# Pre-layernorm attention with an FP8 projection: reciprocals by exp(-ln), pieces spread over rounds, elementwise work on another engine

## Chip, cores and metric

The kernel runs on one core of a Trainium2 chip. The metric is the device time of one execution, in microseconds, as the median of several runs. The engines are named as in the profile: PE (matmul; PEld is its weight load), DVE (vector), ACT (scalar, with activation functions), POOL (GpSimd) and SP, which here only issues DMAs.

## What is computed

Two batches of 2048 rows of 512 numbers pass through attention with 16 query heads and 2 key/value heads of 32 dimensions, with rotary embedding, and then through a projection whose operands are rounded to 8-bit floats. Cut to what matters:

```python
def reference(x, wq, bq, wk, bk, wv, bv, wo, bo, weight):
    h = layernorm(x)
    q, k, v = h @ wq + bq, h @ wk + bk, h @ wv + bv      # 16, 2, 2 heads of 32
    q, k = rope(q) * 32 ** -0.5, rope(k)
    scores = einsum("bqhd,bkhd->bhqk", q, repeat(k)) * 32 ** -0.5
    out = einsum("bhqk,bkhd->bqhd", softmax(scores), repeat(v))
    x = x + out @ wo + bo
    a, sa = quant_e4m3(layernorm(x).reshape(-1, 512))    # one scale for the whole tensor
    w, sw = quant_e4m3(weight)
    return x + (a @ w.T * (sa * sw)).astype(bfloat16)
```

## The kernel before

**Blocks, quads, units, rounds.** The 4096 rows are 8 blocks `n` of 512 rows (4 per batch). A block has 4 quads of heads, and a quad two halves of 256 queries: 64 units `u`, which the main loop takes one after the other. A unit goes over the 2048 keys in 16 chunks of 128, in 4 rounds `r` of 4 chunks. For a chunk `probabilities` (L964 to L988) puts the scores of four heads into one of two PSUM tiles `T` (two matmuls at L978; in the first two chunks four more at L969 subtract the row maxima) and ACT writes `p = exp(T)` (L987). As there are two tiles, the third chunk's matmuls wait for the first chunk's exponential. `weigh` multiplies the probabilities of the *previous* round with the values (L924), so that PE has work between the second and the third chunk.

**Sums of the softmax.** DVE adds the probabilities of two chunks (`add_pair`, L961). The pair of chunks 0 and 1 lies in a `pair` buffer, of which there are two, and an accumulating DMA that POOL issues adds it to the pair of chunks 2 and 3 (`accumulate`, L991). `join` (L994) adds what two rounds left, and PE sums over the keys with a matrix of ones (L942) in the rounds of the next unit. `finish_heads` (L891 to L921) then copies the sums on ACT (L895), takes their maximum for a later check (L897), takes reciprocals in two pieces on DVE (L903) and multiplies on POOL (L904).

**Maxima of the next unit.** In rounds 0 and 1 `first_scores` computes the scores against the first 128 keys and DVE their maxima (L517); in round 3, between the second and the third chunk, `gather_maxima` transposes them on PE and copies them on ACT (`mT`, L533).

**Everything else** is cut into jobs: Python generators that yield the kind of their next step (ON_PE, ON_DVE, OTHER, LATER). Jobs project keys and values of a later block (`project_kv`), queries of the next block (`project_q`), and the output of the previous block (`finish_block`, then `second_norm`). The loop calls `fill(kind, pieces)` at fixed places, which runs the next step of a job that is due: one ON_PE piece in rounds 0 and 1 and two in rounds 2 and 3, as long as there are any. All jobs borrow one PSUM bank (`bank`, `give_back`). Since each engine runs its instructions in the order of the program, a step lands on each engine between the loop's own instructions.

**In a job.** Rotary embedding swaps halves of each head by 8 small DMAs on SP (`swapped`, L304), rotates on DVE two rounds later (`turn`: `rotate`, L309) and multiplies and adds on POOL (`rope`, L325 and L326). `halves` splits a tile into a rounded high part (ACT, L236) and a low part (POOL, L237). For queries this is done in `stack_queries` at the start of a unit, which stores both parts to DRAM and reads them back spread over partitions. The normalisation of a later block's rows is done on ACT with two instructions per tile (L250, L253). `ask` starts the loads of a block at its first unit; where a buffer or a query isn't ready, `take_x` and `stack_next` run further steps at once (`advance`). The bias `bo` is added to the 512 rows of residual by one accumulating DMA of 1 MB on POOL's queue (`add_bias`, L548).

Of the kernel before, what the change touches and what calls it, by code (L numbers as in the profile page):

```python
# [16 lines left out]
P = 128  # L17
# [10 lines left out]
def preln_attn_fp8_ffn_kernel(  # L28
# [54 lines left out]
    LATER = "later"  # L83
    BACK = HB
# [22 lines left out]
    lent = [None]  # L107

# [12 lines left out]
    def give_back():  # L121
        if attending[0]:
            lent[0] = None

# [23 lines left out]
    def load_tables(n):  # L148
        blk = n % NB
        if attending[0] or n == 0:  # L150
            csb = cs.tile([P, 2, TB], F32, tag="cs", name=f"cs_{n}")
        else:
            csb = papool.tile([P, 2, TB], F32, tag="pa", name=f"cs_{n}")
        nc.sync.dma_start(csb[:, 0, :], cos_t[:, blk * TB : (blk + 1) * TB])
        nc.sync.dma_start(csb[:, 1, :], sin_t[:, blk * TB : (blk + 1) * TB])
        return csb
# [28 lines left out]
    def layernorm_stats(src, mean, rstd, name, tiles=range(NT)):  # L185
# [9 lines left out]
        engine = nc.gpsimd if attending[0] else nc.vector  # L195
        engine.tensor_scalar(var[:, at], mv[:, at, 1], EPS, None, ALU.add)
        engine.tensor_copy(mean[:, at], mv[:, at, 0])
# [33 lines left out]

    def halves(src, rows, name):
# [4 lines left out]
        nc.gpsimd.tensor_tensor(lo[:rows], src, hi[:rows].bitcast(F32), ALU.subtract)  # L237
# [6 lines left out]
    def normalized(n, xt, xnT, name):  # L244


        def normalize(i):
            if attending[0]:
                xn = t2(f"xn_{name}_{i}")
                nc.scalar.activation(  # L250
                    xn, xt[:, i, :], AF.Identity, bias=neg_mean[:, i : i + 1]
                )
                nc.scalar.activation(xn, xn, AF.Copy, scale=rstd1[:, n, i : i + 1])  # L253
                return xn
# [12 lines left out]
        if attending[0]:  # L267
            neg_mean = small.tile([P, NT], F32, tag="neg_mean", name=f"neg_mean_{name}")
            nc.scalar.mul(neg_mean, mean1[:, n, :], -1.0)
        for i in range(0, NT, 2):  # L270
            xn = {}
            for h in (i, i + 1):
                yield OTHER if attending[0] else ON_DVE
# [13 lines left out]
    def product(dst, lhs, rhs, chunks=DC):  # L287

        for c in range(chunks):
            yield ON_PE  # L290
# [32 lines left out]
    def rope(dst, q, u, rows, csb):  # L323

        nc.gpsimd.tensor_tensor(q[:rows], q[:rows], csb[:rows, 0, :], ALU.mult)  # L325
        nc.gpsimd.tensor_tensor(dst, u[:rows], q[:rows], ALU.add)  # L326
# [37 lines left out]
    def project_kv(n, xt, xnT, csb):  # L364
# [5 lines left out]
        if b not in vX:  # L370
            vX[b] = wide.tile([P, NTS, GROUPS, HD], F32, tag="vX", name=f"vX_{b}", bufs=2)
        pk = bank(f"pk_{n}")
# [3 lines left out]
        else:  # L376
            nc.gpsimd.tensor_copy(kx[:, :BACK], kx[:, TB:])
# [16 lines left out]
        if attending[0]:  # L394
            beside.insert(0, Job(stack_keys(n, kv, u, csb), due=step[0] + 2))
# [3 lines left out]
    def stack_keys(n, kv, u, csb):  # L399
# [5 lines left out]
        if attending[0]:  # L405
            table_users[0] -= 1
        cols = slice(blk * TB, (blk + 1) * TB)
        yield OTHER
        src = t2(f"dk_{n}")[:KD]
        nc.gpsimd.tensor_tensor(src, kx[:, BACK:], kx[:, :TB], ALU.subtract)  # L410
# [16 lines left out]
    q_raw = {}  # L427

    def project_q(n, xnT, csb):
        for m in range(QUADS):  # L430
            pq = bank(f"pq_{n}_{m}")
# [3 lines left out]
            raw = wide.tile([P, TB], F32, tag="q", name=f"q_{n}_{m}", bufs=QUADS + 1)  # L435
            nc.scalar.activation(raw, pq, AF.Identity, bias=bq_sb[:, m : m + 1])
            give_back()
            if attending[0]:
                u = swapped(raw, P, f"q_{n}_{m}")
                beside.insert(0, Job(turn(n, m, raw, u, csb), due=step[0] + 2))  # L440
            else:
                u = yield from rotated(raw, csb, f"q_{n}_{m}")
                rope(raw, raw, u, P, csb)
                q_raw[n, m] = raw
                table_users[0] -= attending[0]

    def turn(n, m, raw, u, csb):
# [4 lines left out]
        q_raw[n, m] = raw  # L452
# [7 lines left out]
    def stack_queries(k):  # L460

        n, quad = quads[k]
        hi, lo = halves(q_raw.pop((n, quad)), P, f"q_{n}_{quad}")
        qst[k] = wide.tile([P, 4, TB], F32R, tag="qst", name=f"qst_{k}", bufs=2)
        far = dram.tile([P, 2, TB], F32, tag=f"q_far_{k % 2}", name=f"q_far_{k}")
        for h, part in enumerate((hi, lo)):
            nc.sync.dma_start(far[:, h, :], part.bitcast(F32))
        far = far.rearrange("(j d) h t -> d h j t", j=4)
# [77 lines left out]
    def add_bias(xt):  # L546
        rows = bo.partition_broadcast(P).unsqueeze(1).broadcast_to([P, NT, D])
        nc.gpsimd.dma_start(out=xt, in_=rows, accum_op=ALU.add)  # L548

    def add_output(n, xt, attn, i, dims=range(DC)):  # L550

        po = bank(f"po_{n}_{i}_{dims[0]}")
# [135 lines left out]
    with tc.manual_schedule():  # L688
# [16 lines left out]
        assert (0, 0) in q_raw  # L705
# [16 lines left out]
    class Job:  # L722


        def __init__(self, steps, kind=None, due=0, tables=False):
            self.steps = steps
            self.tables = tables
# [8 lines left out]
        def step(self):  # L736
            if self.kind is not None:
                self.tables = False
            self.kind = next(self.steps, None)
            if self.kind == LATER:  # L740
                self.due = step[0] + 1
                self.kind = next(self.steps)

    step = [0]
    NEVER = 10**9
    queue = [Job(q0, ON_PE)]
    owner = [queue[0]]
    table_users[0] = QUADS - sum((0, m) in q_raw or m == 0 for m in range(QUADS))
# [4 lines left out]
    def fill(kind, pieces=1):  # L753

        for _ in range(pieces):
            ready = [job for job in queue if job.due <= step[0] and not job.waits()]
            if lent[0] is not None:
                ready = [job for job in ready if job is owner[0]]
# [16 lines left out]

    seen = const.tile([P, len(units)], F32, tag="seen", name="seen")
    without_x = {}
    x_res = {}
    x_taken, x_done, x_asked = [], set(), set()
# [9 lines left out]
    def take_x(name):  # L789

        while len(x_taken) >= 3 and x_taken[-3] not in x_done:
            advance()
        x_taken.append(name)

# [4 lines left out]
    def later(project, n, x, *makes):  # L799
# [3 lines left out]
        table_users[0] = QUADS if project is project_q else 1  # L803
        csb = load_tables(n)
        yield from project(n, x, *made, csb)
# [3 lines left out]
    def stack_next(u):  # L809
# [3 lines left out]
        if half == 0:  # L813
            if k + 1 < len(quads) and k + 1 not in qst:
                while quads[k + 1] not in q_raw:
# [17 lines left out]
    def start(job):  # L833
        job.due = step[0] + 1

    def load_residual(n):
        x_res[n] = xpool.tile([P, NT, D], F32, tag="x", name=f"x_res_{n}")
        load_by_halves(x_res[n], x_in[n], lambda: unbiased.append(n))
# [6 lines left out]

    def ask(u):

        k, half = units[u]

        for m in unbiased:  # L850
            add_bias(x_res[m])
            biased.add(m)
            if m in without_x:
                without_x.pop(m).due = step[0] + 2
        unbiased.clear()
        n, quad = quads[k]
        if half == 0 and quad == 0:
# [567 lines left out]
```

## Time and profile before

| | |
|---|---|
| median of 3 runs | 1808.78 us (1807.12 to 1813.49) |
| profiled execution | 1806.86 us, span of its instructions 1805.0 us |
| before the first exponential of the loop | 98 us |
| main loop, 64 units | 98 to 1689 us |
| after the loop (scale, 8-bit projection, output) | 1690 to 1805 us |
| granted TensorE clock, mean | 0.966 (0.99 in the loop) |
| busy in 98:1690 of 1592 us | PE 1485, ACT 1126, DVE 1178, POOL 509 us |

An engine's row in a timeline gives its start, its length, the engine, the source line, the operation, the tile written and read, shapes and count; in brackets stands how long the engine was idle before it, and what ended that. A row of the groups gives the number of instructions, then their busy time in us and the mean length of one in ns, then the idle time before them by what ended it.

### The profile page before, as it was taken

The page shows a single profiled execution, that of the slowest core. Times are in us where ns is not written, and L with a number is a line of the kernel's source. Part 1 is how long each engine was busy: PE and PEld are TensorE (multiplying, and loading weights), DVE is VectorE, ACT ScalarE, POOL GpSimd, SP SyncE. Part 2 cuts the span into 40 slices and gives each one's busy share as a digit, 9 for nine tenths or more (in the row PEclk, how much of TensorE's full clock was granted, in tenths as well). Part 3 has the DMA queues.
Part 4 walks back from the last instruction along what each step waited for, and adds up shares of the span by engine and source line. Part 5 has one row for each costly group of instructions (what it writes and reads, how often), then busy time and mean ns, then how long its engine had stood idle before and what let it go on. Part 6 is the DMA issues. An engine that isn't in the chain of part 4 may idle for free.

```text
span 1805.0 us, 33804 instructions
## 1 busy us (share of the span) xinstructions
PE 1598.6 (89%) x13483; PEld 916.2 (51%) x13483; DVE 1315.7 (73%) x1526; ACT 1208.3 (67%) x1473; POOL 545.2 (30%) x552
## 2 busy tenths in 40 slices
PE   5588999899998999898999998999899988899664
PEld 3254555555555555555555554555555545555322
DVE  4547787767876787767768777787878787577697
ACT  2167677876767776776766777767777667566365
POOL 2333333244322532243314222332324223122100
PEclk9699999999999999999999999999999999999878
DMA  5676676767577866767588567766677558776222
GB/s 187 175 165 134 155 151 152 179 147 158 119 189 168 171 131 150 196 157 160 121 206 167 123 141 175 161 145 128 135 186 155 120 132 182 146 183 140 64 82 107
DMA packets 105431, 272.65 MB, mean 151 GB/s; under 512 B 15536, under 2 KB 16176, under 8 KB 102576
## 3 DMA queue, kind: packets, MB, share of 16 engines
q0 software_dynamic: 40944, 142.10, 42.1%
q1 hardware_dynamic: 61904, 126.92, 23.3%
q8 instruction: 108, 1.77, 0.4%
q10 hardware_dynamic: 2416, 1.38, 0.2%
q14 instruction: 59, 0.48, 0.1%
HBM read 87.36 MB, written 40.89 MB: 71 GB/s over the span
## 4 chain that ended last, share of the span: by engine, by line
PE 50%; DVE 14%; DMA 12%; issue 10%; ACT 7%; POOL 4%; SPq 2%; ACTq 0%; DVEq 0%; POOLq 0%
PE T L978 17%; PE avs L924 16%; DMA pa<-pa 9%; ACT p L987 6%; PE po L291 5%; DVE pa L961 4%; PE pq L291 3%; PE avs L942 2%; PE T L969 2%; DVE pa L994 2%; SPq L304 2%; DMA sw_q<-q 2%; PE pk L291 2%; PE s L509 1%; DVE v L229 1%
## 5 line engine op out<-in xcount | busy, mean ns | idle before, releaser
L987 ACT ACTIVATE p<-T 128x1024 f32<-128x1024 f32 x1024 | 991.9, 1023 | 218.1 <-PE T L978 214.3
L961 DVE TENSOR_TENSOR pa<-p,p 128x1024 f32<-128x1024 f32 x511 | 687.6, 1348 | 383.0 <-ACT p L987 273.2
L978 PE MATMUL T<-qst,dkS 128*128 128x512 f32 x2048 | 688.2, 446 | 44.8 <-ACT p L987 44.4
L991 POOL DMA_DIRECT2D pa<-pa x255 | 221.0, 867 | 971.8 <-DVE pa L961 671.6
L924 PE MATMUL avs<-p,vX 128*32 128x256 f32 x8192 | 497.3, 383 | 0.0
L978 PEld LDWEIGHTS T<-qst,dkS 128*128 128x128 f32 x2048 | 343.7, 191 | 285.2 <-ACT p L987 157.6
L924 PEld LDWEIGHTS avs<-p,vX 128*32 128x32 f32 x8192 | 240.4, 110 | 228.0 <-issue 96.5
L994 DVE TENSOR_TENSOR pa<-pa,pa 128x1024 f32<-128x1024 f32 x125 | 169.8, 1358 | 0.0
L291 PE MATMUL po<-wo_sb,attn 128*128 128x512 f32 x256 | 126.1, 604 | 0.0
L903 DVE RECIPROCAL both<-both 128x128 f32<-128x128 f32 x128 | 121.4, 949 | 5.6 <-DVE seen L897 0.5
L969 PE MATMUL T<-mT,sel 128*128 128x256 f32 x512 | 102.7, 324 | 11.2 <-ACT p L987 10.7
L291 PE MATMUL pq<-xnT_q,wq_sb 128*128 128x512 f32 x224 | 112.1, 607 | 0.0
L942 PE MATMUL avs<-pa,ones 128*32 128x256 f32 x1048 | 81.5, 385 | 28.7 <-DVE pa L994 27.7
L969 PEld LDWEIGHTS T<-mT,sel 128*128 128x128 f32 x512 | 78.0, 193 | 46.0 <-issue 20.6
L509 PEld LDWEIGHTS s<-dkS,qst 128*128 128x128 f32 x512 | 79.0, 196 | 22.2 <-DVE mx L517 10.9
L517 DVE TENSOR_REDUCE mx<-s 128x4 f32<-128x512 f32 x128 | 87.4, 683 | 2.8 <-PE s L509 2.8
L1012 ACT COPY both<-avs 128x256 f32<-128x256 f32 x64 | 23.9, 373 | 90.8 <-PE avs L942 88.1
L509 PE MATMUL s<-dkS,qst 128*128 128x128 f32 x512 | 74.4, 269 | 9.4 <-DVE mx L517 9.4
L904 POOL TENSOR_TENSOR attn<-both 128x256 f32<-128x256 f32 x64 | 78.9, 1232 | 9.7 <-DVE both L903 9.7
L895 ACT COPY both<-avs 128x256 f32<-128x256 f32 x64 | 23.9, 373 | 84.8 <-PE avs L942 84.8
L326 POOL TENSOR_TENSOR q<-sw_q,q 128x512 f32<-128x512 f32 x30 | 54.7, 1825 | 38.3 <-DVE sw_q L309 37.9
L533 ACT CAST mT<-mtp 128x256 fp32r<-128x256 f32 x64 | 23.8, 372 | 56.5 <-PE mtp L529 56.5
(124 smaller groups left out, 1075.5 us busy)
## 6 DMA issues: line engine op xcount, KB each, us to landing
pa<-pa POOLq DMA_DIRECT2D x255, 512.0 KB, 5.0
qst<-q_far SPq DMA_DIRECT2D x128, 256.0 KB, 4.9
q_far<-hi_q SPq DMA_DIRECT2D x32, 256.0 KB, 2.8
q_far<-lo_q SPq DMA_DIRECT2D x32, 256.0 KB, 3.4
x_res<-in_L_attn_x_dram SPq DMA_DIRECT2D x16, 512.0 KB, 7.2
x_res<-in_L_attn_bo_dram POOLq DMA_DIRECT2D x8, 1024.0 KB, 12.7
out_dram<-v SPq DMA_DIRECT2D x16, 512.0 KB, 2.8
sw_q<-q SPq DMA_DIRECT2D x240, 32.0 KB, 3.6
```

The costliest lines, as they stand in the source:

```text
L291: nc.tensor.matmul(dst, lhs(c), rhs(c), start=(c == 0), stop=(c == chunks - 1))
L509: nc.tensor.matmul(s[:, j, :], qst[k][:, j, at : at + P], stacked["dkS"][:, group(k), :FIRST], start=True, stop=True, skip_group_check=True,)
L517: nc.vector.tensor_reduce(mx[:, i, :], s, AX.X, ALU.max)
L903: nc.vector.reciprocal(piece, piece)
L924: nc.tensor.matmul(av[j * HD : (j + 1) * HD, :], vX[batch(k)][:, kc, group(k), :], p[:, j, :], start=(kc == 0), stop=(kc == NTS - 1), tile ...
L942: nc.tensor.matmul(dst[j * HD : (j + 1) * HD, :], ones, part[:, j, :], start=start and i == 0, stop=stop and i == len(parts) - 1, tile_pos ...
L961: nc.vector.tensor_tensor(pa, a, b, ALU.add)
L969: nc.tensor.matmul(T[:, j, :], sel[:, j, :], maxima[u], start=(j % 2 == 0), stop=True, skip_group_check=True,)
L978: nc.tensor.matmul(T[:, j : j + 2, :], stacked["dkS"][:, group(k), kc * P : (kc + 1) * P], qst[k][:, j : j + 2, half * HB : (half + 1) * H ...
L987: nc.scalar.activation(p, T, AF.Exp, scale=SCALE)
L991: nc.gpsimd.dma_start(out=to, in_=of, accum_op=ALU.add)
L994: nc.vector.tensor_tensor(to, to, of, ALU.add)
```

## The change

Reciprocals: ACT copies the sums and adds them up in the same instruction (`accum_out`), then computes ln and exp of the negated result as a first guess; DVE makes one Newton step with three instructions, of which the last multiplies with the values. The steps are at least a round apart.

Jobs: a `product` no longer yields ahead of its first matmul, its callers do. `pieces` hands out one ON_PE piece in a round, and two in rounds 2 and 3 when more is owed than the rest of the block's rounds hold. No piece of a product starts in the round in which the bank was given back. An ON_DVE step may run while another job holds the bank.

Engines: within the loop rope, low halves, key differences, the statistics' small steps and the normalisation go to DVE (the normalisation as one instruction); before the loop POOL keeps them.

Loads: one list of what is wanted and from which unit on, two units ahead of the block; a load is taken when a buffer is free, and nothing is advanced for it. Tables of a key job lie in the tile of its normalised rows and are loaded after the transposes; tables of a query job are loaded with its first query. Queries are split and stored when they have been turned (`put_away`), a round later; `stack_queries` only reads. The bias goes to each of a block's four row tiles by a DMA of 256 KB.

Buffers: `pair` 3 for 2, `q` 2 for 5, `both` 3 rows for 2.

```diff
+            given[0] = step[0]
...
-    def load_tables(n):
+    def load_tables(n, of=None):
         blk = n % NB
-        if attending[0] or n == 0:
+        if of is not None:
+            csb = wide.tile([P, 2, TB], F32, tag=of, name=f"cs_kv_{n}")
+        elif attending[0] or n == 0:
...
+    def elementwise():
+
+        return nc.vector if attending[0] else nc.gpsimd
...
-        nc.gpsimd.tensor_tensor(lo[:rows], src, hi[:rows].bitcast(F32), ALU.subtract)
+        elementwise().tensor_tensor(lo[:rows], src, hi[:rows].bitcast(F32), ALU.subtract)
...
             if attending[0]:
                 xn = t2(f"xn_{name}_{i}")
-                nc.scalar.activation(
-                    xn, xt[:, i, :], AF.Identity, bias=neg_mean[:, i : i + 1]
-                )
-                nc.scalar.activation(xn, xn, AF.Copy, scale=rstd1[:, n, i : i + 1])
-                return xn
...
         for c in range(chunks):
-            yield ON_PE
+            if c > 0:
+                yield ON_PE
...
-        nc.gpsimd.tensor_tensor(q[:rows], q[:rows], csb[:rows, 0, :], ALU.mult)
-        nc.gpsimd.tensor_tensor(dst, u[:rows], q[:rows], ALU.add)
+        elementwise().tensor_tensor(q[:rows], q[:rows], csb[:rows, 0, :], ALU.mult)
+        elementwise().tensor_tensor(dst, u[:rows], q[:rows], ALU.add)
...
+            csb = load_tables(n, "xnT")
             beside.insert(0, Job(stack_keys(n, kv, u, csb), due=step[0] + 2))
...
-            raw = wide.tile([P, TB], F32, tag="q", name=f"q_{n}_{m}", bufs=QUADS + 1)
+            raw = wide.tile([P, TB], F32, tag="q", name=f"q_{n}_{m}", bufs=2)
...
+                if csb is None:
+                    yield TABLES
+                    table_users[0] = QUADS
+                    csb = load_tables(n)
                 u = swapped(raw, P, f"q_{n}_{m}")
...
-        q_raw[n, m] = raw
+        yield LATER
+        yield OTHER
+        put_away(n, m, raw)
+
+    q_far = {}
+
+    def put_away(n, m, raw):
+
+        far = dram.tile([P, 2, TB], F32, tag=f"q_far_{n % 2}_{m}", name=f"q_far_{n}_{m}")
+        for h, part in enumerate(halves(raw, P, f"q_{n}_{m}")):
+            nc.sync.dma_start(far[:, h, :], part.bitcast(F32))
+        q_far[n, m] = far
...
-        rows = bo.partition_broadcast(P).unsqueeze(1).broadcast_to([P, NT, D])
-        nc.gpsimd.dma_start(out=xt, in_=rows, accum_op=ALU.add)
+        nc.gpsimd.dma_start(out=xt, in_=bo.partition_broadcast(P), accum_op=ALU.add)
...
-                ready = [job for job in ready if job is owner[0]]
+                ready = [job for job in ready if job is owner[0] or job.kind == ON_DVE]
+            if kind == ON_PE and given[0] == step[0]:
+                ready = [job for job in ready if job.kind != ON_PE]
...
+    def pieces(u, r, ending_soon):
+
+        if ending_soon:
+            return 2
+        left = QUADS * HALVES - 2 - u % (QUADS * HALVES)
+        owed = sum(job.products for job in queue)
+        return 2 if r >= 2 and owed > (ROUNDS + r - 2) * left else 1
...
+    def add_some_bias():
+
+        if unbiased and unbiased[0][2] <= step[0]:
+            n, i, _ = unbiased.pop(0)
+            add_bias(x_res[n][:, i, :])
+            if i == NT - 1:
+                biased.add(n)
+                if n in without_x:
+                    without_x.pop(n).due = step[0] + 2
...
+    for n in range(NBLK):
+        early = max(0, n * PER_BLOCK - 2)
+        if NB + n < NBLK:
+            wanted.append((early, load_keys, f"kv_{NB + n}", NB + n))
+        if n + 1 < NBLK:
+            wanted.append((early, load_queries, f"q_{n + 1}", n + 1))
+        if n > 0:
+            wanted.append((early, load_residual, f"res_{n - 1}", n - 1))
+    wanted.append((early, load_residual, f"res_{n}", n))
...
-        nc.scalar.copy(both[:, 1, :], sums)
+        av, total, guess = (both[:, i, :] for i in range(3))
+        nc.scalar.activation(total, sums, AF.Copy, accum_out=seen[:, u : u + 1])
+        yield LATER
         yield ON_DVE
-        nc.vector.tensor_reduce(
-            seen[:, u : u + 1], both[:, 1, :].bitcast(U32), AX.X, ALU.max
-        )
-        for c in range(HB // P):
-            yield ON_DVE
-            piece = both[:, 1, c * P : (c + 1) * P]
-            nc.vector.reciprocal(piece, piece)
-        nc.gpsimd.tensor_tensor(
-            attn_of[n][:, quad, half * HB : (half + 1) * HB], both[:, 0, :], both[:, 1, :], ALU.mult
+        nc.scalar.activation(guess, total, AF.Ln)
+        nc.scalar.activation(guess, guess, AF.Exp, scale=-1.0)
+        yield LATER
+        yield ON_DVE
+        nc.vector.tensor_tensor(total, total, guess, ALU.mult)
+        nc.vector.scalar_tensor_tensor(total, total, 2.0, guess, ALU.subtract, ALU.mult)
+        nc.vector.scalar_tensor_tensor(
+            attn_of[n][:, quad, half * HB : (half + 1) * HB], av, -1.0, total, ALU.mult, ALU.mult
         )
...
-            bufs=4 if far else 2,
+            bufs=4 if far else 3,
...
+                load_wanted(u)
                 load_some()
...
+                add_some_bias()
...
-                fill(ON_PE, 1 if r < HT and not ending_soon else 2)
+                fill(ON_PE, pieces(u, r, ending_soon))
```

## The prediction

> **What bounds the kernel now.** I read the page's busy shares first, then its chain, then the groups of instructions with shapes kept apart, then the timeline of ACT, PE and DVE in a plain unit and in the slow stretches.
>
> ```profile
> span 1805.0 us, 33804 instructions
> PE 1598.6 (89%) x13483; PEld 916.2 (51%) x13483; DVE 1315.7 (73%) x1526; ACT 1208.3 (67%) x1473; POOL 545.2 (30%) x552
> PE 50%; DVE 14%; DMA 12%; issue 10%; ACT 7%; POOL 4%; SPq 2%; ACTq 0%; DVEq 0%; POOLq 0%
> L987 ACT ACTIVATE p<-T 128x1024 f32<-128x1024 f32 x1024 | 991.9, 1023 | 218.1 <-PE T L978 214.3 <-DVE pa L961 3.8
> L961 DVE TENSOR_TENSOR pa<-p,p 128x1024 f32<-128x1024 f32 x511 | 687.6, 1348 | 383.0 <-ACT p L987 273.2 <-DMA pa<-pa 105.2 <-ACT both L1012 1.1
> ```
>
> PE is 89% busy and fills half of the chain, but L987 shows the partner: of ACT's idle time before the exponentials, 214 us ended with PE, while PE in turn waits for ACT to empty one of two T banks. The loop is a ping-pong of PE (T) and ACT (exp). One round (four exponentials) of a plain unit, ACT first, then PE at its end:
>
> ```profile
> 706.50 1.94 ACT L987 ACTIVATE p<-T 128x1024 f32<-128x1024 f32 x2 [0.30 <-PE T L978]
> ...
> 712.68 1.94 ACT L987 ACTIVATE p<-T 128x1024 f32<-128x1024 f32 x2 [0.70 <-PE T L978]
> 715.30 0.37 ACT L533 CAST mT<-mtp 128x256 fp32r<-128x256 f32 x1 [0.69 <-PE mtp L529]
> 715.83 1.94 ACT L987 ACTIVATE p<-T 128x1024 f32<-128x1024 f32 x2 [0.15 <-PE T L978]
> 718.94 1.94 ACT L987 ACTIVATE p<-T 128x1024 f32<-128x1024 f32 x2 [1.17 <-PE T L978]
> ...
> 716.03 1.88 PE L291 MATMUL po<-wo_sb,attn 128*128 128x512 f32 x4
> 717.34 1.03 PE L969 MATMUL T<-mT,sel 128*128 128x256 f32 x4
> ```
>
> This fourth round lasts 718.94 - 712.68 = 6.26 us. ACT is idle 0.69 + 0.15 us between the second and third exponential; the third ends at 716.85 (715.83 + 1.02) and PE starts the next unit's T at 717.34, 0.49 us later. So ACT's slack there is 1.33 us, and no more. Taking every round's start from the same timeline (252 rounds of 63 units), the medians for rounds without and with projection pieces are 5.81/6.13 (first), 5.29/5.37 (second), 5.79/6.19 (third, two pieces), 5.99/6.27 us (fourth, two): 22.9 us per unit without pieces, 24.0 with six. Pieces are nearly free, so their even spread by itself is worth little. The units took 24.88 us on average; the rounds' excess over their medians sums to 79 us, in some 25 rounds. That is what the change can win. Where it sits:
>
> ```profile
> 739.64 0.73 ACT L250 ACTIVATE xn_kv<-x_kv,neg_mean_kv 128x512 f32<-128x512 f32 x1
> 740.47 0.72 ACT L253 ACTIVATE xn_kv<-xn_kv,rstd 128x512 f32<-128x512 f32 x1
> 741.10 0.71 ACT L250 ACTIVATE xn_kv<-x_kv,neg_mean_kv 128x512 f32<-128x512 f32 x1
> 741.85 0.72 ACT L253 ACTIVATE xn_kv<-xn_kv,rstd 128x512 f32<-128x512 f32 x1
> 742.47 0.35 ACT L533 CAST mT<-mtp 128x256 fp32r<-128x256 f32 x1
> ...
> 1547.45 2.36 DVE L961 TENSOR_TENSOR pa<-p,p 128x1024 f32<-128x1024 f32 x2 [11.88 <-DMA pa<-pa]
> ...
> 980.25 1.83 DVE L309 SCALAR_TENSOR_TENSOR sw_q<-sw_q,sign,cs 128x512 f32<-128x512 f32 x1 [4.27 <-DMA sw_q<-q]
> ...
> 955.13 3.68 DVE L961 TENSOR_TENSOR pa<-p,p 128x1024 f32<-128x1024 f32 x1
> ...
> 954.96 1.53 POOL L237 TENSOR_TENSOR lo_q<-q,hi_q 128x512 fp32r<-128x512 f32 x1
> ```
>
> Three kinds: the normalisation on ACT with eight transposes, in four fourth rounds (8.5, 11.8, 11.8, 12.3 us against 6.27: 19 us); one round of 13.4 us where DVE waited 11.9 us for an accumulating DMA beside the 1 MB bias (8 us); and the rest, 52 us, where DVE comes late because it waits for the swapped query (4.27 us at 980) or is held up while POOL computes (a pair addition of 3.68 us at 955, beside L237 on POOL).
>
> **The change, part by part.**
>
> *Reciprocal by exp(-ln).* The list of the built program's instructions has, on ACT, 129 loads of a function set where before has one; in 61 of the 64 units they stand like this, between the second and third exponential of a fourth round, ahead of the mT copy:
>
> ```
> L1028 Activation p_13
> L939 LoadActFuncSet
> L939 Activation both<-both 128x256     (Ln)
> L940 LoadActFuncSet
> L940 Activation both<-both 128x256     (Exp)
> L544 TensorCopy mT
> L1028 Activation p_14
> ```
>
> The trace of before prices one load and one 256-wide ACT instruction:
>
> ```profile
> L282 ACT ACT_TABLE_LOAD x1 | 1.3, 1283 | 9.9 <-DMA wkv_sb<-in_L_attn_wv_dram 9.9
> L1012 ACT COPY both<-avs 128x256 f32<-128x256 f32 x64 | 23.9, 373 | 90.8 <-PE avs L942 88.1 <-POOL ends L579 1.3 <-POOL q L326 1.3
> L903 DVE RECIPROCAL both<-both 128x128 f32<-128x128 f32 x128 | 121.4, 949 | 5.6 <-DVE seen L897 0.5
> ```
>
> Inserted: 2 x 1.283 + 2 x 0.373 = 3.31 us. Behind it on ACT wait mT, two exponentials, and so PE's next T. In the plain round: second exponential ends at 714.62, + 3.31 + 0.37 (mT) + 1.02 = 719.32, third exponential done; PE's T starts then instead of at 717.34, and the next exponential 1.60 us after it (718.94 - 717.34) at 720.92. Round: 8.24 us. Against the mean fourth round of 6.13 us (half-way between 5.99 and 6.27, since the change leaves 0 to 2 pieces there) that is +2.1 us, 63 times in the loop: **+132 us**. Nothing covers it: PE is in order, and its pieces are used up before it reaches T. Bounds: if the neighbours overlap as back-to-back exponentials do (2 x 1.023 - 1.94 = 0.1 us each, 0.36 in all), +1.75, 110 us; if each of the four borders costs a smallest ACT instruction (L269, 0.2 us), +2.9, 183 us. I take 3.31, as the load's own row has no such addition.
>
> The Trainium skill, "ScalarE: Activation LUTs", section "What ACT_TABLE_LOAD costs", gives about 2.66 us for a switch, 1.28 of load and 1.38 of drain. The row above agrees with its load; no run here shows the drain. By it the sum would be higher by 2 x 1.38 x 63 = 174 us, an estimate from that page.
>
> What it takes from DVE (121.4 us of reciprocals and 26.4 us of maxima) and from POOL (78.9 us at L904) lay beside PE and ACT: nothing on the path. The three Newton steps, about 0.41 us each by the 128x256 row of L897, put 79 us back on DVE, which has 414 us idle in the loop (1592 - 1178). They run a round or more later; `both` has a row more and the same two buffers, last read in the round in which the next but one is written: no new wait. The last unit's chain after the loop was 0.37 + 0.41 + 2 x 0.95 + 1.23 = 3.9 us and becomes 0.37 + 3.31 + 3 x 0.41 = 4.9: **+1 us**.
>
> *Work off POOL and off ACT.* Rope, low halves and key differences go to DVE: 90 of 128x512 at 0.69 us (L320) and some 16 of 64x512 at no more, 73 us, and 16 normalisations of 0.55 us (L257). With Newton and without the reciprocals DVE gains 161 + 9 - 156 = about 14 us, less what L961 loses beside POOL (1348 ns mean against 1.23 us in the plain unit, 511 times: 60 us). The ACT normalisation (2 x 11.6 us) goes. The 19 us of the first kind should go whole, as the transposes now stand four to a round.
>
> *Third pair buffer, bias by row tiles.* DVE's 105 us of waits for accumulations end mostly beside PE (ACT's wait for DVE is 3.8 us in all); they count where DVE was really late: the 8 us round. POOL issues 32 bias transfers instead of 8 (0.87 us each by L991 instead of 1.73: +14 us, in an engine 70% idle), of a quarter of the bytes each, so less stands ahead of an accumulation. Taken: **-27 us** with the first kind; bounds 0 and -27.
>
> *The rest of the excess.* Of the 52 us, 17.8 us are DVE's waits for the swapped query (6 of 30 rotations), which stay: the rotation is still due two rounds later, behind eight SP transfers. Taken: **-34 us**; bounds 0 and -52.
>
> *Earlier loads, no forced advancing, queries stored when made.* The same bytes move; 64 stores of query halves are issued earlier on SP, and 11 pairs of tables (7 for queries, 4 for keys) now just ahead of their first use, four of them behind the store of xnT. A rotation that waits for them blocks DVE, and the pair additions behind it. By the mean of the rotations now, 17.8/30 = 0.6 us, for 11 first uses: **+7 us**; bounds 0 and 11 x 4.5 = 50 us.
>
> Sum: 1805 + 132 + 1 - 27 - 34 + 7 = 1884 us of span; around it lay 1.9 us (1806.86 - 1805.0): **1886 us**. The profiled execution stood 0.1% under the median of 1808.78, which I don't correct for.
>
> **Rivals.** *The loads don't cost* (faster). If Ln and Exp were served without a switch, 0.75 us would be inserted, under the slack of 1.33: 1886 - 132 = 1754 us. It decides where the insertion is below about 2.2 us (1.33 of slack and 53/63 of what is won), that is with one load of 1.28 us or less per unit. The Trainium skill, "ScalarE: Activation LUTs", section "Table sets: the hidden batching unit", names a set with both functions, by which one load would do for the whole kernel. The instruction list speaks against this rival: a load ahead of every Ln and of every such Exp. 9%, of which 3% for one load per unit: 2.03 us inserted, 0.8 x 63 = 50 us, which the 53 us won cancel.
>
> *A switch is dearer than its row* (slower still): the load waits until ACT has nothing in flight and the next instruction starts cold. Priced by one full exponential (1.02 us) per load, 5.35 us are inserted, the round takes 10.3 us, 4.15 x 63 = 261 us: 2015 us. For it: the only load in the trace stands alone before an idle ACT, so its row hides this. Against: no other pair of ACT instructions shows such a gap. 10%.
>
> *The excess isn't won* (slower): DVE, with rope at its head and tables that have just been asked for, stalls as before: 1805 + 132 + 1 + 7 to 50 + 2 = 1947 to 1990 us. For it: DVE's longest waits are for sw_q, which stay. 15%.
>
> **Chances.** The forecast 66%, with its own range from 1839 (all 79 us won, 110 inserted, no new wait) to 1937 us (183 inserted). I record 1835 to 1990, which takes in the excess not won; what lies outside is the fast rival and the dear switch, 19%. Within 0.3%, about what a measurement here can tell from no change: 3%; faster 6%; slower 91%.
>
> **What would show it.** 129 ACT_TABLE_LOAD rows of about 1.28 us; fourth rounds of 8.2 us and the others as before; PE idle before the next unit's T at L1010, ended by ACT p; no L250/L253 rows; DVE's wait for pa<-pa far below 105 us. I am wrong if fourth rounds stay near 6.2 us, or if ACT shows gaps around its loads.

## The result, and the profile after

The changed kernel takes **1883.0 us** (median of 4 runs, 1878.9 to 1888.3) against 1808.0 us before: ratio 1.040, 95% interval 1.037 to 1.043. It is slower by 75 us; 1886 us were forecast. The total came out right by luck: two of its terms were wrong, and their errors nearly cancel. The loads of function sets cost more than I said, and the rest of the change wins more.

The page of the changed kernel: span, busy shares, and the chain by engine and line.

```profile
span 1877.0 us, 33364 instructions
PE 1619.6 (86%) x13478; PEld 916.1 (49%) x13483; DVE 1250.3 (67%) x1673; ACT 1397.2 (74%) x1757; POOL 318.1 (17%) x381
PE 54%; ACT 19%; issue 11%; DVE 10%; DMA 4%; POOL 1%; SPq 1%; ACTq 0%; DVEq 0%; POOLq 0%
PE T L1019 18%; PE avs L965 17%; ACT p L1028 11%; PE T L1010 4%; PE po L292 4%; ACT L939 4%; PE pq L292 3%; PE avs L983 3%; PE s L520 2%; PE pk L292 1%; DVE pa L1002 1%; ACT both L939 1%; ACT both L940 1%; DVE v L233 1%; SPq L305 1%
```

ACT's share of the chain went from 7% to 19%, and L939 is on it. DVE and POOL are less busy, and DMA fell from 12% to 4% of the chain: what the change set out to relieve is relieved. The groups, which answer to L987, L961 and the single load of before; the last row is the kernel before's for L1010:

```profile
L1028 ACT ACTIVATE p<-T 128x1024 f32<-128x1024 f32 x1024 | 994.7, 1025 | 176.7 <-PE T L1019 173.9
L1002 DVE TENSOR_TENSOR pa<-p,p 128x1024 f32<-128x1024 f32 x511 | 624.9, 1223 | 501.8 <-ACT p L1028 500.9
L939 ACT ACT_TABLE_LOAD x64 | 82.1, 1283 | 1.1
L940 ACT ACT_TABLE_LOAD x64 | 82.1, 1283 | 1.1
L1010 PE MATMUL T<-mT,sel 128*128 128x256 f32 x512 | 98.5, 320 | 116.0 <-ACT p L1028 115.5
...
L969 PE MATMUL T<-mT,sel 128*128 128x256 f32 x512 | 102.7, 324 | 11.2 <-ACT p L987 10.7 <-ACT vX L389 0.5
```

There are 128 more loads of 1283 ns, with 1.1 us of idle time before 64 of them in all: they stand back to back with their neighbours. The pairs of loads lie in 61 fourth rounds, in two third rounds, and once after the loop. PE waits 115.5 us for ACT at L1010, the first matmuls of a unit's T (10.7 us before). DVE's wait for accumulations, 105 us before, is gone from L1002, whose mean fell from 1348 to 1223 ns. One plain fourth round, on ACT and then at its end on PE:

```profile
882.67 1.94 ACT L1028 ACTIVATE p<-T 128x1024 f32<-128x1024 f32 x2 [0.70 <-PE T L1019]
884.63 1.28 ACT L939 ACT_TABLE_LOAD   x1
885.92 0.42 ACT L939 ACTIVATE both<-both 128x256 f32<-128x256 f32 x1
886.36 1.28 ACT L940 ACT_TABLE_LOAD   x1
887.65 0.42 ACT L940 ACTIVATE both<-both 128x256 f32<-128x256 f32 x1
887.97 0.35 ACT L544 CAST mT<-mtp 128x256 fp32r<-128x256 f32 x1
888.23 1.94 ACT L1028 ACTIVATE p<-T 128x1024 f32<-128x1024 f32 x2
890.56 1.97 ACT L1028 ACTIVATE p<-T 128x1024 f32<-128x1024 f32 x2 [0.39 <-PE T L1019]
...
886.03 1.88 PE L292 MATMUL po<-wo_sb,attn 128*128 128x512 f32 x4
889.31 0.74 PE L1010 MATMUL T<-mT,sel 128*128 128x256 f32 x4 [1.40 <-ACT p L1028]
...
890.35 0.64 PE L1010 MATMUL T<-mT,sel 128*128 128x256 f32 x4
...
891.40 1.93 PE L965 MATMUL avs<-p,vX 128*32 128x256 f32 x32
```

From 884.63 to 887.97, 3.34 us, lie between the second exponential and the mT copy (3.31 forecast). PE's T starts 889.31 - 882.67 = 6.64 us into the round, to the hundredth as worked out; then the next exponential comes after 1.25 us, not 1.60, so the round lasts 7.89 us and not 8.24. This is no single lucky round: in all 61 fourth rounds with loads PE's T starts 6.62 to 6.67 us after the round's first exponential.

For every kernel below the starts of the rounds' first exponentials give this table, from one profiled execution each (us; the loop goes from the start of the first exponential to the end of the last, the means are over all 64 units, and "half clock" counts the stretches within the loop in which the records grant PE 0.5 of its clock):

| kernel | time, median | first exp at | loop | mean round 1, 2, 3, 4 | half clock: stretches, us |
|---|---|---|---|---|---|
| before | 1808.0 | 98.4 | 1590.5 | 6.22, 5.59, 6.41, 6.64 | 10, 41 |
| after | 1883.0 | 104.6 | 1653.1 | 6.39, 5.48, 6.03, 7.93 | 20, 68 |
| e1_recip | 1729.6 | 104.9 | 1508.1 | 6.15, 5.54, 5.91, 5.96 | 1, 3 |
| e2_expexp | 1727.4 | 105.3 | 1503.5 | 6.07, 5.52, 5.99, 5.92 | 0, 0 |
| e3_before_ln | 1956.3 | 97.7 | 1738.5 | 6.46, 5.55, 6.81, 8.35 | 28, 119 |
| e4_double | 2197.5 | 102.6 | 1968.3 | 7.24, 5.45, 6.16, 11.90 | 64, 393 |
| e5_busy | 1850.9 | 105.1 | 1629.3 | 6.06, 5.47, 6.07, 7.86 | 1, 3 |
| e6_double_busy | 2150.7 | 102.5 | 1918.8 | 6.07, 5.48, 6.12, 12.31 | 2, 14 |
| e8_double_busy5 | 2084.7 | 102.6 | 1855.5 | 6.24, 5.46, 6.15, 11.14 | 10, 41 |
| e7_best | 1721.5 | 94.9 | 1504.0 | 6.17, 5.49, 5.88, 5.97 | 1, 7 |
| e9_pool | 1781.8 | 96.0 | 1565.6 | 6.57, 5.88, 6.04, 5.97 | 12, 44 |
| e10_act_norm | 1733.8 | 97.6 | 1514.5 | 6.04, 5.73, 5.78, 6.13 | 2, 7 |
| e11_two_pairs | 1776.9 | 96.4 | 1558.5 | 6.26, 5.58, 6.53, 5.98 | 6, 27 |
| e12_front | 1734.6 | 96.5 | 1519.7 | 6.07, 5.45, 6.19, 6.04 | 2, 10 |

### The profile page after: what moved, and what is told of

It is laid out like the page before. It is cut to its first block, busy times and chain, and to the rows that moved or that the text cites. A ratio compares the mean times of both kernels' runs of the same rounds, so it can differ in the third digit from the quotient of the medians.

```text
span 1877.0 us, 33364 instructions
## 1 busy us (share of the span) xinstructions
PE 1619.6 (86%) x13478; PEld 916.1 (49%) x13483; DVE 1250.3 (67%) x1673; ACT 1397.2 (74%) x1757; POOL 318.1 (17%) x381
## 3 DMA queue, kind: packets, MB, share of 16 engines
q10 hardware_dynamic: 2416, 1.38, 0.2%
## 4 chain that ended last, share of the span: by engine, by line
PE 54%; ACT 19%; issue 11%; DVE 10%; DMA 4%; POOL 1%; SPq 1%; ACTq 0%; DVEq 0%; POOLq 0%
PE T L1019 18%; PE avs L965 17%; ACT p L1028 11%; PE T L1010 4%; PE po L292 4%; ACT L939 4%; PE pq L292 3%; PE avs L983 3%; PE s L520 2%; PE pk L292 1%; DVE pa L1002 1%; ACT both L939 1%; ACT both L940 1%; DVE v L233 1%; SPq L305 1%
## 5 line engine op out<-in xcount | busy, mean ns | idle before, releaser
L1002 DVE TENSOR_TENSOR pa<-p,p 128x1024 f32<-128x1024 f32 x511 | 624.9, 1223 | 501.8 <-ACT p L1028 500.9
L965 PE MATMUL avs<-p,vX 128*32 128x256 f32 x8192 | 504.4, 387 | 0.0
L965 PEld LDWEIGHTS avs<-p,vX 128*32 128x32 f32 x8192 | 242.5, 111 | 237.4 <-issue 108.8
L1010 PE MATMUL T<-mT,sel 128*128 128x256 f32 x512 | 98.5, 320 | 116.0 <-ACT p L1028 115.5
L1035 DVE TENSOR_TENSOR pa<-pa,pa 128x1024 f32<-128x1024 f32 x125 | 152.2, 1218 | 19.6 <-DMA pa<-pa 19.6
L1010 PEld LDWEIGHTS T<-mT,sel 128*128 128x128 f32 x512 | 80.5, 212 | 170.8 <-ACT p L1028 161.3
L1053 ACT COPY both<-avs 128x256 f32<-128x256 f32 x64 | 23.9, 373 | 95.0 <-PE avs L983 95.0
L939 ACT ACT_TABLE_LOAD x64 | 82.1, 1283 | 1.1
L940 ACT ACT_TABLE_LOAD x64 | 82.1, 1283 | 1.1
L936 ACT ACTIVATE both<-avs 128x256 f32<-128x256 f32 x64 | 24.7, 386 | 66.5 <-PE avs L983 66.5
L292 PEld LDWEIGHTS po<-wo_sb,attn 128*128 128x128 f32 x256 | 44.3, 190 | 19.9 <-issue 11.2
L292 PEld LDWEIGHTS pq<-xnT_q,wq_sb 128*128 128x128 f32 x224 | 39.4, 190 | 17.4 <-issue 13.5
```

What stands on the lines that cost most here:

```text
L292: nc.tensor.matmul(dst, lhs(c), rhs(c), start=(c == 0), stop=(c == chunks - 1))
L939: nc.scalar.activation(guess, total, AF.Ln)
L940: nc.scalar.activation(guess, guess, AF.Exp, scale=-1.0)
L965: nc.tensor.matmul(av[j * HD : (j + 1) * HD, :], vX[batch(k)][:, kc, group(k), :], p[:, j, :], start=(kc == 0), stop=(kc == NTS - 1), tile ...
L1002: nc.vector.tensor_tensor(pa, a, b, ALU.add)
L1010: nc.tensor.matmul(T[:, j, :], sel[:, j, :], maxima[u], start=(j % 2 == 0), stop=True, skip_group_check=True,)
```

## The experiments

### The loads: taken out, without their instructions, alone, twice

**e1_recip** puts DVE's reciprocals in place of ln, exp and Newton:

```diff
...
-        nc.scalar.activation(guess, total, AF.Ln)
-        nc.scalar.activation(guess, guess, AF.Exp, scale=-1.0)
-        yield LATER
-        yield ON_DVE
-        nc.vector.tensor_tensor(total, total, guess, ALU.mult)
-        nc.vector.scalar_tensor_tensor(total, total, 2.0, guess, ALU.subtract, ALU.mult)
-        nc.vector.scalar_tensor_tensor(
-            attn_of[n][:, quad, half * HB : (half + 1) * HB], av, -1.0, total, ALU.mult, ALU.mult
+        for c in range(HB // P):
+            piece = total[:, c * P : (c + 1) * P]
+            nc.vector.reciprocal(piece, piece)
+            yield ON_DVE
+        nc.vector.tensor_tensor(
+            attn_of[n][:, quad, half * HB : (half + 1) * HB], av, total, ALU.mult
         )
...
```

> The changed kernel with DVE's reciprocals (two of 128x128) in place of ln, exp and the Newton steps; all else as changed. Theory (the two function-set loads sit between the second and third exponential of a fourth round and push PE's next T): the 62 fourth rounds fall from 7.9 to about 6.15 us, the other rounds stay, so 1883 - 62 x 1.75 = about 1775 us, faster than before by some 2%. Rival (the new reciprocals cost little and the other edits lose): stays at 1860 to 1885 us.

Measured: 1729.6 us, 0.958 of before (0.956 to 0.960). The direction of the theory, but larger: 153 us below the changed kernel where 108 were expected. Fourth rounds fell from 7.93 to 5.96 us, 126 us over the loop, and first rounds from 6.39 to 6.15, 15 us. By the table's executions the loops differ by 145 us in all.

**e2_expexp** keeps all instructions, but not the switch:

```diff
-        nc.scalar.activation(guess, total, AF.Ln)
+        nc.scalar.activation(guess, total, AF.Exp, scale=0.001)
```

> The changed kernel with Exp (of a thousandth of the sum) in place of Ln, so that the same two ACT instructions and Newton steps run but no function set changes; the factor is then not a reciprocal and the output not the reference's. Theory (the loads, not the two instructions): 0.84 us inserted where ACT has 1.33 us of slack, so no loss: 1770 to 1785 us, fourth rounds about 6.2 us. Rival (two more ACT instructions and a late Newton step are what costs): fourth rounds near 7 us or more, 1830 us and above.

Measured: 1727.4 us, 0.958 (0.955 to 0.961), fourth rounds 5.92 us. With as many ACT instructions and the same Newton steps, and no loads, the loss is gone: it is the 128 loads that cost 156 us. DVE's reciprocals in e1_recip cost no more than what stands here in their place: the two kernels are 2 us apart. It also shows that 0.8 us more on ACT hide in the fourth round, as the slack of 1.33 us said.

**e3_before_ln** makes this one edit in the kernel before:

```diff
-        nc.scalar.copy(both[:, 1, :], sums)
...
-            nc.vector.reciprocal(piece, piece)
...
+        nc.scalar.activation(total, sums, AF.Copy, accum_out=seen[:, u : u + 1])
...
+        nc.scalar.activation(guess, total, AF.Ln)
+        nc.scalar.activation(guess, guess, AF.Exp, scale=-1.0)
...
+        nc.vector.tensor_tensor(total, total, guess, ALU.mult)
...
```

> The kernel before with only the reciprocals changed to exp(-ln) and the Newton steps (and the sum in place of the maximum). Theory: each unit pays 1.75 us as in the changed kernel, 64 x 1.75 = 112: about 1920 us. Rival (the loads fall into waits that the kernel before has anyway, such as the slow rounds): 1860 us or less.

Measured: 1956.3 us, 1.083 (1.080 to 1.086): +151 us on the 1805.5 us of before in the same comparison, not +112. The toll is as large as in the changed kernel, but it lies elsewhere: by the table's means fourth rounds lose 109 us (126 in the changed kernel), third rounds 26 (6.41 to 6.81) and first rounds 15. So some of it may hide in the slow fourth rounds of before, as the rival had it, but the third rounds lose as much again; why they do is not shown.

**e4_double** runs ln and exp twice in the changed kernel:

```diff
-        nc.scalar.activation(guess, total, AF.Ln)
-        nc.scalar.activation(guess, guess, AF.Exp, scale=-1.0)
+        for _ in range(2):
+            nc.scalar.activation(guess, total, AF.Ln)
+            nc.scalar.activation(guess, guess, AF.Exp, scale=-1.0)
```

> The changed kernel with the pair of ln and exp run twice, so four loads per unit in place of two. Theory (no slack is left, each further us on ACT is a us of the unit): another 2 x 1.283 + 2 x 0.42 = 3.4 us, 62 x 3.4 = 211, about 2094 us. Rival (part of it hides behind other waits): below 2030 us; rival (a switch costs more than its row, which back to back would show as gaps): above 2150 us.

Measured: 2197.5 us, 314 us more than the changed kernel where 211 were expected. The number falls on the side of the dearer switch, but the records don't: the loads show no gaps (2.3 us of idle time before each line's 128), and first rounds, which hold none, went from 6.39 to 7.24 us. The granted clock points to a cause. Three stretches of e4_double follow: PE's wait, the 3.5 us after it, the next 5.5 us. A row gives the stretch, its length, the busy time of PE, PEld, DVE, ACT and POOL (with the number of instructions), the granted clock, and two numbers on DMA.

```profile
1018.00:1024.90 6.90, 2.20 (x7) 0.81 (x5) 1.30 (x2) 6.80 (x11) 0.00 (x0) 0.82 1.04 214
1025.00:1028.50 3.50, 3.44 (x12) 2.87 (x12) 1.83 (x2) 1.94 (x3) 0.86 (x1) 0.50 0.78 273
1028.50:1034.00 5.50, 5.50 (x53) 3.05 (x53) 2.44 (x5) 3.34 (x4) 0.00 (x0) 0.94 0.52 98
```

The clock is the third number from the end. After a wait of 4.9 us PE gets 0.50 for the time in which it has to make the next T. The changed kernel has it too, after a wait of 1.79 us; the columns are the same:

```profile
1166.00:1171.00 5.00, 3.21 (x18) 2.06 (x15) 1.89 (x3) 4.96 (x8) 0.00 (x0) 1.00 1.06 259
1171.00:1174.40 3.40, 3.40 (x23) 2.06 (x26) 1.45 (x2) 2.39 (x3) 0.86 (x1) 0.50 0.34 61
1174.40:1179.00 4.60, 4.60 (x45) 2.77 (x35) 2.41 (x5) 2.35 (x4) 0.00 (x0) 1.00 0.67 135
```

and the matmuls that run there, on PE's timeline:

```profile
1170.01 0.74 PE L1010 MATMUL T<-mT,sel 128*128 128x256 f32 x4 [1.79 <-ACT p L1028]
1170.59 0.69 PE L1019 MATMUL T<-qst,dkS 128*128 128x512 f32 x2
1171.08 1.06 PE L1010 MATMUL T<-mT,sel 128*128 128x256 f32 x4
1171.93 1.05 PE L1019 MATMUL T<-qst,dkS 128*128 128x512 f32 x2
1172.92 2.66 PE L965 MATMUL avs<-p,vX 128*32 128x256 f32 x32
```

At 1170.01 four matmuls take 0.74 us, at 1171.08 the same four 1.06; the 32 at L965 take 2.66 us. In the plain round above, the second four of L1010 took 0.64 us and the 32 at L965 1.93. So I formed a second theory: the loads cost their time on ACT, and then again because PE, having waited, is slowed.

### The clock: PE kept busy while it waits

**e5_busy** gives PE two matmuls in the wait whose results nobody reads; **e6_double_busy** and **e8_double_busy5** do the same with eight and five in the kernel of e4_double.

```diff
                 fill(ON_PE, pieces(u, r, ending_soon))
+                if last and before and not ending_soon:
+                    for _ in range(2):
+                        nc.tensor.matmul(
+                            before.avs.rearrange("p a t -> p (a t)"),
+                            wq_sb[:, 0, :P],
+                            wq_sb[:, 0, :],
+                            start=True,
+                            stop=True,
+                            skip_group_check=True,
+                        )
```

> The changed kernel with two matmuls of 128x512 that nobody reads (into the finished half of a sums tile), at the end of each fourth round, where PE waits for ACT some 1.4 us or more. Theory (part of the loss is the granted clock: in the changed kernel 19 of the 22 first rounds that follow a PE wait show 0.5 for 3.4 us when the wait was over 1.6 us, none of 23 when it was shorter): more work on PE, but fewer stretches at 0.5 (28 after 100 us, about 9 of them after the loop; here under 15), fourth rounds still 7.9 us, first rounds 6.15 us on average in place of 6.39: 1850 to 1870 us. Rival (the clock has nothing to do with the wait): the same stretches, and 1883 us or more, as PE does 62 us more work.

Measured: 1850.9 us, 1.024 (1.022 to 1.025): 32 us faster than the changed kernel (24 us between the loops of the table, one execution each) with 122 matmuls more, and one stretch at half clock in the loop in place of 20. First rounds went to 6.06 us, fourth rounds stayed (7.86). The expectation miscounts the trace: of the 40 waits over 1.6 us (not 22) 19 were followed by half clock.

```profile
1153.49 1.88 PE L1119 MATMUL avs<-wq_sb 128*128 128x512 f32 x4
1155.45 0.74 PE L1010 MATMUL T<-mT,sel 128*128 128x256 f32 x4
1156.03 0.63 PE L1019 MATMUL T<-qst,dkS 128*128 128x512 f32 x2
1156.49 0.63 PE L1010 MATMUL T<-mT,sel 128*128 128x256 f32 x4
```

The two (four records, 1.88 us) fill the wait, and the second four of L1010 take 0.63 us.

> The kernel with the pair of ln and exp run twice, with eight such matmuls at the end of each fourth round (about 4.2 of the 4.9 us that PE waits). Theory: the loads alone cost 3.4 us per unit more than the changed kernel, and what came on top there (2197.5 - 1883 - 211 = 104 us) is the clock at 0.5 in the round that follows: 2075 to 2110 us, first rounds back from 7.3 to about 6.2 us. Rival (a second switch simply costs more): 2180 us or above.

Measured: 2150.7 us, outside both ranges. The half clock is gone (2 stretches for 64, first rounds 6.07 us), but fourth rounds rose to 12.31 us: eight of these matmuls (16 records) take longer than the 4.9 us that PE would wait, as its timeline shows:

```profile
1028.40 7.03 PE L1120 MATMUL avs<-wq_sb 128*128 128x512 f32 x16
```

The same with five, e8_double_busy5:

> As the last kernel with ln and exp twice, but five unread matmuls per unit in place of eight, since one of them took 0.88 us (7.03 us for eight) and not 0.53 as assumed, so that eight outlasted the wait. Theory: with the clock kept at full, two more loads and their two instructions cost 3.4 us in each fourth round and nothing elsewhere: 1851 + 61 x 3.4 = about 2058 us (2045 to 2075), fourth rounds 11.3 us. Rival (a second switch costs more than its row): above 2100 us.

Measured: 2084.7 us, between the two. Fourth rounds are 11.14 us on average over the 64 units, 3.28 above e5_busy: 64 x 3.28 = 210 of the 234 us. That is 3.44 us for each of the 61 fourth rounds that hold loads, where 3.4 were forecast for two more loads and their instructions. In these 61 rounds PE's next T starts 10.08 to 10.13 us into the round, 3.45 us later than the 6.64 of the changed kernel. Ten stretches at half clock are left, and the first rounds have 11 us more than e5_busy; 6 us came after the loop. A switch costs its row and no more.

### What the rest of the change wins

**e7_best** is e1_recip with the first two queries split where they are first stacked:

```diff
...
-                put_away(n, m, raw)
+                unsplit[n, m] = raw
...
+        if (n, quad) in unsplit:
+            put_away(n, quad, unsplit.pop((n, quad)))
...
```

The wait that it is to remove, in the changed kernel ahead of the loop:

```profile
63.91 0.62 ACT L244 CAST hi_q<-q 128x512 fp32r<-128x512 f32 x1 [3.90 <-POOL q L327]
```

> The changed kernel with DVE's reciprocals, and the first two queries split when they are first stacked, as before, and not at once. Theory (before the loop, ACT's copy of the high half waits for POOL's rope and holds the copies behind it): first exponential at 98 us in place of 105, so 1729.6 - 6 = about 1723 us. Rival (something else of the changed order delays the start): 1728 us or more.

Measured: 1721.5 us, 0.952 (0.951 to 0.954), the fastest kernel here, 86 us below the one before. The first exponential comes at 94.9 us. Each of the four kernels that follow undoes one part in it.

**e9_pool** (`elementwise` returns POOL in the loop too):

```diff
-        return nc.vector if attending[0] else nc.gpsimd
+        return nc.gpsimd
```

> The fastest kernel so far (DVE's reciprocals, 1721.5 us) with rope, low halves and key differences back on POOL within the loop. Theory (the prediction's third kind: DVE is held up while POOL computes, and comes late with the pair sums that PE waits for): a third to all of the 34 us come back: 1735 to 1755 us, L1002-like pair additions near 1.35 us in place of 1.22. Rival (DVE has time to spare, nothing waits for it): 1718 to 1726 us.

Measured: 1781.8 us, 60 us lost, more than the theory gave. First rounds are 6.57 us and second rounds 5.88 (6.17 and 5.49). Two kinds of rows of e9_pool, the pair additions and a wait, and last the pair additions of e7_best:

```profile
L1003 DVE TENSOR_TENSOR pa<-p,p 128x1024 f32<-128x1024 f32 x511 | 663.6, 1299 | 396.0 <-ACT p L1029 394.0
ACT hi_q L244 <- POOL q L327: 40.7, 16, 4.2
...
L1003 DVE TENSOR_TENSOR pa<-p,p 128x1024 f32<-128x1024 f32 x511 | 623.7, 1221 | 331.9 <-ACT p L1029 329.2 <-DMA pa<-pa 1.3
```

The pair additions take 1299 ns for 1221 in e7_best; and where queries are split a round after they are turned, ACT's copy of the high half waits for POOL, 40.7 us in 16 places, and the exponentials stand behind it. The second is a wait that the kernel before didn't have, so not all of the 60 us are won by this part; how they divide is not shown.

**e10_act_norm** (two ACT instructions per tile again, handed out as OTHER steps):

```diff
+                nc.scalar.activation(
+                    xn, xt[:, i, :], AF.Identity, bias=neg_mean[:, i : i + 1]
+                )
+                nc.scalar.activation(xn, xn, AF.Copy, scale=rstd1[:, n, i : i + 1])
+                return xn
...
-                yield ON_DVE
+                yield OTHER if attending[0] else ON_DVE
...
```

> The fastest kernel so far with the normalisation of later blocks on ACT again (16 tiles, two instructions of 0.72 us each). Theory (23 us of ACT work between exponentials, beyond the slack where two tiles fall into one place; the prediction gave 19 us for it together with the bunched transposes): 1733 to 1745 us. Rival (the loss before came from eight transposes in one round, which stay spread here): below 1727 us.

Measured: 1733.8 us, +12 us, at the near edge of what the theory gave.

**e11_two_pairs**:

```diff
-            bufs=4 if far else 3,
+            bufs=4 if far else 2,
...
```

> The fastest kernel so far with two pair buffers in place of three. Theory (DVE's waits for the accumulating DMA lie beside PE except where the bias stood in the same queue; with the bias in quarters little is left): 1721 to 1728 us. Rival (the third buffer is what brings the gain): 1740 us or more, DVE's wait for pa<-pa again near 100 us.

Measured: 1776.9 us, +55 us: the rival. Third rounds went from 5.88 to 6.53 us. Waits of e11_two_pairs (total us, times, longest):

```profile
DVE pa L1003 <- DMA pa<-pa: 109.2, 45, 6.2
PE avs L984 <- DVE pa L1036: 39.2, 27, 5.2
```

and the same two of e7_best:

```profile
PE avs L984 <- DVE pa L1036: 5.8, 8, 1.1
DVE pa L1003 <- DMA pa<-pa: 1.3, 1, 1.3
```

The kernel before has this wait of PE too, 27.7 us of it; the changed kernel keeps 6.2:

```profile
L942 PE MATMUL avs<-pa,ones 128*32 128x256 f32 x1048 | 81.5, 385 | 28.7 <-DVE pa L994 27.7 <-DMA pa<-pa 0.9
L983 PE MATMUL avs<-pa,ones 128*32 128x256 f32 x1048 | 80.5, 382 | 6.3 <-DVE pa L1035 6.2
```

The pair addition waits for the DMA that still reads its buffer, the `join` behind it on DVE comes late, and PE, in order, waits for the join at L984, in the third round in 25 of the 27 cases. DVE's wait is not beside PE, it is handed on to it through the join. PE's waits there are 33 us longer than in e7_best, of the 55 us; the rest is not traced to rows.

**e12_front** hands out the projection pieces as before (that none starts in the round in which the bank was given back stays):

```diff
-                fill(ON_PE, pieces(u, r, ending_soon))
+                fill(ON_PE, 1 if r < HT and not ending_soon else 2)
```

> The fastest kernel so far (1721.5 us) with the old hand-out of projection pieces: one in the first two rounds and two in the last two, as long as there are any, in place of an even spread. Theory (the prediction: pieces are nearly free, 24.0 us a unit with six and 22.9 without, and the time is linear in them): 1715 to 1728 us. Rival (the even spread carries part of the gain): 1735 us or more.

Measured: 1734.6 us, ratio to before 0.960 (0.958 to 0.963) where e7_best has 0.952 (0.951 to 0.954): 13 us, between the two ranges. The even spread is worth something, mostly in third rounds (6.19 for 5.88 us).

## Why the prediction was right, and where it was not

- **The place and price of a load: right.** 128 loads, back to back, 3.34 us inserted for 3.31, PE's next T at the hundredth forecast, and within 0.03 us of it in all 61 rounds. The dear switch, a rival at 10%, is out: 1.1 us of idle time before each line's 64 loads, and two more loads with their instructions cost 3.44 us a round in e8_double_busy5. The Trainium skill, "ScalarE: Activation LUTs", section "What ACT_TABLE_LOAD costs", adds a drain of 1.38 us to each switch; these rows show none.
- **The round of 8.24 us: a little too long.** The term "the next exponential 1.60 us after it" was taken from a round in which PE came without a wait; after one it is 1.25. But the round without loads is 5.96, not 6.13, so the difference nearly holds: fourth rounds lost 126 us in all, 2.07 us for each of the 61 that hold loads, where I had 2.1.
- **"63 times in the loop: +132" as the whole toll: too small.** The runs give 153 to 156 us (e1_recip, e2_expexp; 151 in the kernel before). The step that failed is that PE only waits: 19 stretches at half clock follow its waits at the start of a unit, and with PE kept busy the kernel is 32 us faster (e5_busy). Without the half clock the loads cost 1850.9 - 1729.6 = 121 us.
- **"DVE's 105 us of waits for accumulations end mostly beside PE": wrong.** I read it from ACT's direct wait for DVE, 3.8 us, and overlooked the way over `join` to PE's sums, which a row of the kernel before showed (27.7 us at L942; 6.2 us are left of it after the change). Undoing the third buffer costs 55 us.
- **The excess: "-27", "-34" and "+7", 54 us net; measured 76** (e1_recip against 1805.5 us of before in the same comparison), and that after 6.5 us lost ahead of the loop, which I had not seen coming: a copy on ACT that waits for POOL (first exponential 104.9 for 98.4 us; e7_best has 94.9). In the loop e1_recip wins 82 us, all of the 79 us of excess over the medians: the bound, not the value that I took. The rotations' new waits for tables didn't come. DVE's gain of "about 14 us" has two terms wrong: by the rows named there it is 79 + 73 + 9 = 161 us more and 121 + 26 = 148 us less, 13 us; it names no row for a second 9 or for 156. Of the first kind, 19 us, the normalisation itself is 12 us (e10_act_norm).
- **"Pieces are nearly free": roughly.** 13 us of 1722.
- **The sum.** Loads about 21 us too cheap, gains about 22 us too small: the forecast of 1886 came within 3 us of 1883 because they offset each other, which is luck. Its sign rested on the loads, and e2_expexp shows that alone: without them the same kernel is 0.958 of before.
- **The fast rival** (9%) named the right alternative: with no switch 1754 us were worked out, 1727 measured. Only the instruction list told the two apart.

What stays open: how much each part wins in the kernel before. The parts undone in e7_best add up to more (60 + 55 + 12 + 13 us) than they win together, since a part that is missing also brings waits and half clock that the others hide; parts alone in the kernel before were not tried. The bias in quarters was not undone by itself.

## What to carry to other kernels

Before pricing an activation by its own row, read in the built program which function set each one is served from; two functions that no common set was chosen for cost two loads each time they alternate: here 153 us, in place of reciprocals whose 121 us on DVE lay beside the critical path. A wait on the critical engine can cost twice, once as a wait and once in the clock that is granted after it. And an engine's wait is only free when whoever waits for its *next* instructions has slack too.

## What the runs showed of the hardware that I had not expected

- **PE's clock falls after short waits.** In the changed kernel, at the start of a unit: after waits up to 1.6 us in none of 23 cases, from 1.6 to 2.0 us in 5 of 22, from 2.0 to 2.6 us in 2 of 4, above in 12 of 14, the records grant 0.5 of the clock, mostly for 3.4 us. The Trainium skill, "TensorE: Matmul & The Clock Gate", part 1, lowers the clock after an idle window of about 3.4 us; here waits of 1.79 us were enough, so PE need not be idle for that long. A wait's length alone doesn't decide it, and the clock records show what does. In each of the 14 traces all stretches at half clock begin on one grid of 3.413 us, whatever the waits do. In the loops, PE had less than 1.4 us of busy time in 126 cells of that grid not themselves at half clock, and half clock followed each of them; it followed 33 of the 92 cells with 1.4 to 1.9 us, and none of the 6302 with more. So it counts how much of a wait falls into one cell.
- **Useless matmuls made the kernel faster**, by 32 us, as they kept the clock at full.
- **The sum in the copying instruction isn't free**, as it is a second one on ACT (0.20 us); what it costs the kernel was not tested by itself:

```profile
L936 ACT ACTIVATION_READ_ACCUMULATOR both<-avs 128x1 f32 x64 | 12.4, 195 | 0.0
```
